# Switch experts in a two-layer transformer kernel: block inputs transposed one block ahead, outputs stored by slot and gathered by token, and an attention stage that starts from half of its operands

## The chip, the cores and the metric

The kernel runs on one core of one Trainium2 chip. The metric is the device time of one execution in microseconds (us). The core's engines are named as the profile names them: PE (TensorE, matmul and transpose), PEld (its weight loads), DVE (VectorE), ACT (ScalarE), POOL (GpSimd, which also issues the indirect DMAs) and SP (SyncE, which here only issues DMAs). L942 is line 942 of the kernel before.

## The reference, cut to what matters

The input x is [4, 1024, 128] (four images of 1024 tokens), all in float32. Two layers follow one another, each with two residual steps:

```python
x = x + L0_attn(layernorm(x))   # causal attention, 16 heads, rotary and content parts
x = x + L0_ffn(layernorm(x))    # "first experts"
x = x + L1_attn(layernorm(x))   # "second attention": 38 fixed offsets from 0 to 192
x = x + L1_ffn(layernorm(x))    # "last experts": top 2 of 8, rotations, a gate

def L0_ffn(x):                  # x is [4096, 128] here; 8 experts, FFN = 512
    route = softmax(x @ router_w + router_b)
    max_prob, max_ind = max(route), argmax(route)
    for e in range(8):
        a, g = split(x @ w1[e], 2)           # each 512 wide
        y = silu(a) * g @ w2[e]
        out = where(max_ind == e, y, out)
    return out * max_prob

def L1_attn(x):                 # 16 heads of 8
    q, k, v = x @ Wqkv.T + bqkv
    scores = q . k[n - offset] * scale + pos_bias[offset, head]
    out = softmax(scores) . v[n - offset]    # offsets before the start are left out
    return out * sigmoid(x @ Wgate.T + bgate) @ Wout.T + bout
```

## The kernel before

**Tiles.** x stays in SBUF for the whole program as 32 tiles of 128 tokens (P = 128, B = 4 images, NB = 8 tiles in an image, NT = 32). The four stages run one after the other: the first attention (to about 1150 us of the profiled span), the first experts (1150 to 1353 us), the second attention (to about 2000 us) and the last experts. In the stages that matter here PE executes its instructions in the order in which the program writes them (`manual_schedule`); the order on the other engines is set by the framework's scheduler when the program is built. Every engine executes its own instructions in order, so one that waits holds up all behind it.

**Sorting.** A token goes to one expert only. `route(t0, t1, room, ps_1)` sorts the tokens of the tiles t0 to t1 by expert into blocks of 128 slots in which all slots have the same expert. There are two groups, tiles 0 to 24 and 24 to 32 (`SORTED`); as each expert's share is rounded up to whole blocks, the first group has 24 + 7 = 31 blocks and the second 8 + 7 = 15, together 46. `route` is a generator: it normalises tokens (half of the tiles on DVE, half on POOL), transposes them on PE, stores them in DRAM (`xn_d`), computes the router's logits, and leaves `src_i` (for every slot the row of its token), `ex_i` (the expert of every block) and, inside it, `pos` (for every token its slot). The first group is sorted beside the first attention, the second one in pieces beside the first blocks.

**Blocks.** The stage's loop runs over the blocks j, with three of them in flight:

- `front(j)`: an indirect DMA on POOL gathers the block's 128 tokens from xn_d into xg (L932, 6 buffers); PE transposes xg (L937); DVE copies the transpose to xgT (L939); PE's sequencer loads the expert's number into a register (L940); PE multiplies xgT with the two halves of that expert's w1 into pa (L942) and pg (L949); ACT takes the silu of pa (sa, L947); DVE multiplies it with pg (hw, L954).
- `back(j)`, first half, one iteration later: PE transposes hw (L964) and ACT copies it to hT (L968). Second half, two iterations later: PE multiplies with w2 into y (L972), DVE copies y to ys (L978, 4 buffers), and an indirect DMA on POOL scatters ys to the rows of y_d that belong to its tokens (L979).

Between these, `piece()` runs one piece of the work in `aside`: first the sorting of the second group, then `tables()`, which loads what the second attention needs (by_query, by_key: 32 loads on SP, and weights), and, from the iteration after which the first group is complete, `outputs(b)` for the images 0 to 2. `outputs(b)` loads the 1024 rows of y_d of an image in order of tokens into yg (one DMA of 512 KB on SP, L1065) and adds yg times the router's probability (`mp`) to x on DVE, in eight instructions (L1074).

**Second attention.** Its work is cut into 16 units (b, g): image b, and a group g of four heads. `operands(n)` makes queries and keys of unit n. For the first unit of an image it begins with `shared(b)`: the layer norm's statistics, the normalised tokens xn (POOL, L1263), their transposes (PE L1267, copied to xnT by DVE L1268), the addition of b_out to x (POOL, L1271), the gate (L1279, L1280) and the values (L1284, L1288). Then come four matmuls (L1313), with qT (L1318) and kT (L1324) written by ACT. `maxima(n)` computes, in 16 steps, the scores sc (PE L1343) from which DVE takes the largest of every query (L1350); `turn` transposes these maxima (L1359, L1361, L1364). `attend(n)` computes the scores again with keys on the partitions (st, L1426), adds the bias (DVE L1435, sb), exponentiates (ACT L1439, pt) and multiplies with the values (av, L1451).

Ahead of the loop over the units, the program makes all operands of unit 0, then runs 22 steps of maxima (16 of unit 0, `lead` = 6 of unit 1). Beside these, the operands of unit 1 are made from the fifth step on, and the outputs of the first experts of the last image (`last`) are fetched and added from the seventh on:

```python
for _ in operands(0):
    pass
making = operands(1)
...
while done_m < steps + lead:
    if done_m >= 6:
        next(last, None)
    if done_m >= 4:
        for _ in making:
            break
```

Of the kernel before, what the change touches and what calls it, by code (L numbers as in the profile page):

```python
# [10 lines left out]
F32 = mybir.dt.float32  # L11
# [88 lines left out]
def fused_layers(ctx: ExitStack, tc: tile.TileContext, a: dict, out: bass.AP):  # L100
# [139 lines left out]

    mp = const.tile([P, NT], F32, tag="mp", name="mp")
    routed = []

    def route(t0, t1, room, ps_1):
# [4 lines left out]
        y_d = tc.dram_tile([1 + nt * P, D], F32, name=f"y_d{t0}")  # L249
        src_i = const.tile([P, nblk], I32, tag=f"src_i{t0}", name=f"src_i{t0}")  # L250
        ex_i = const.tile([P, nblk], I32, tag=f"ex_i{t0}", name=f"ex_i{t0}")
        inslot, idblk = room([P, nt, P], BF16), room([P, nt, 2, nblk], BF16)
# [13 lines left out]
        xna, xnT = room([P, 4, D]), room([P, 512])  # L266
        none = xna[0:1, 0, :]
# [3 lines left out]
        for b in range(t0 // NB, t1 // NB):  # L271
# [5 lines left out]
            for g in range(NB // 4):  # L277
                for q in range(4):
# [5 lines left out]
                yield  # L284
# [10 lines left out]
                yield  # L295
# [19 lines left out]
            nc.vector.reciprocal(mp[:, til], mp[:, til])  # L315

# [41 lines left out]
        pos_i = room([P, nt], I32)  # L358
# [35 lines left out]
        for g in range(nt // 4):  # L394
# [5 lines left out]
            yield  # L400
# [12 lines left out]
        routed.append((nblk, src_i, ex_i, xn_d, y_d))  # L413
# [503 lines left out]
    with ph0 as ph:  # L917
# [7 lines left out]

        def front(j):

            g = int(j >= routed[0][0])
            src_i, ex_i, xn_d = routed[g][1:4]
            k = j - g * routed[0][0]  # L930
            xg = pw.tile([P, D], F32, tag="xg", bufs=6)
            nc.gpsimd.indirect_dma_start(  # L932
                out=xg[:, :], out_offset=None, in_=xn_d[:, :],
                in_offset=bass.IndirectOffsetOnAxis(ap=src_i[:, k : k + 1], axis=0),
            )
            ps = ps_1.tile([P, 512], F32, tag="ps1")
            nc.tensor.transpose(ps[:, :P], xg, ident)  # L937
            xgT = pw.tile([P, P], F32, tag="xgT", bufs=3)
            nc.vector.tensor_copy(xgT, ps[:, :P])  # L939
# [17 lines left out]
        def back(j, hw, e):  # L957

            g = int(j >= routed[0][0])
            src_i, _, _, y_d = routed[g][1:]  # L960
            k = j - g * routed[0][0]
# [9 lines left out]
            for f in range(NFC):  # L971
# [7 lines left out]
            nc.gpsimd.indirect_dma_start(  # L979
                out=y_d[:, :], out_offset=bass.IndirectOffsetOnAxis(  # L980
                    ap=src_i[:, k : k + 1], axis=0
                ),
                in_=ys[:, :], in_offset=None,
            )
            yield

# [109 lines left out]
        for j in range(total + 2):  # L1096
            if j == first - 1:
                while len(routed) < 2:
                    piece()
# [634 lines left out]
```

## Time and profile before

| what | value |
|---|---|
| three runs | 2224.97, 2225.94, 2228.13 us; median 2225.94 us |
| profiled execution | 2226.58 us, its span 2224.8 us |
| mean granted clock of PE | 0.978 of full speed |
| busy share of the span | PE 92%, DVE 60%, PEld 49%, ACT 42%, POOL 20% |
| instructions | 31832 |
| DMA | 49.84 MB in 52836 packets |

By stage, in us of the span:

| stage | from, to | length | PE busy | DVE busy | POOL busy | granted clock |
|---|---|---|---|---|---|---|
| first attention, second half | 700 to 1150 | 450 | 431.5 | 232.4 | 93.1 | 0.99 |
| first experts | 1150 to 1353 | 203 | 170.8 | 79.1 | 92.7 | 0.96 |
| from there to the first st | 1353 to 1403 | 50 | 36.8 | 26.3 | 16.3 | 0.86 |
| second attention | 1403 to 2000 | 597 | 568.1 | 472.2 | 67.6 | 0.98 |
| last experts | 2000 to 2224.8 | 224.8 | 210.1 | 104.6 | 33.1 | 0.98 |

The profile is of one execution. "Busy" counts the time in which an engine executes instructions; a wait is put down to the instruction that waited and to the event that ended the wait, which is inferred from semaphores. The granted clock is the share of full speed that the chip's throttle allowed PE.

### The profile page before, as it was taken

The page shows a single profiled execution, that of the slowest core. Times are in us where ns is not written, and L with a number is a line of the kernel's source. Part 1 is how long each engine was busy: PE and PEld are TensorE (multiplying, and loading weights), DVE is VectorE, ACT ScalarE, POOL GpSimd, SP SyncE. Part 2 cuts the span into 40 slices and gives each one's busy share as a digit, 9 for nine tenths or more (in the row PEclk, how much of TensorE's full clock was granted, in tenths as well). Part 3 has the DMA queues.
Part 4 walks back from the last instruction along what each step waited for, and adds up shares of the span by engine and source line. Part 5 has one row for each costly group of instructions (what it writes and reads, how often), then busy time and mean ns, then how long its engine had stood idle before and what let it go on. Part 6 is the DMA issues. An engine that isn't in the chain of part 4 may idle for free. (4 is left out here: it accounts for less than half of the span.)

```text
span 2224.8 us, 31832 instructions
## 1 busy us (share of the span) xinstructions
PE 2048.0 (92%) x11540; PEld 1085.6 (49%) x11540; DVE 1345.9 (60%) x4098; ACT 923.8 (42%) x1491; POOL 443.8 (20%) x641
## 2 busy tenths in 40 slices
PE   5888999999999999999988887999999999989997
PEld 3654444444444444445335553555555555544453
DVE  5676746565555655555314343878778788674453
ACT  1112243344433444334543333454555545464553
POOL 3111122013210223013134543010000000151111
PEclk9999999999999999999999998999999999899998
DMA  3000000000000000020113220000000000031220
GB/s 68 1 1 1 1 2 1 2 1 1 1 1 1 1 1 1 6 79 28 36 37 109 77 56 18 2 1 2 2 1 2 1 2 2 13 97 55 86 82 15
DMA packets 52836, 49.84 MB, mean 22 GB/s; under 512 B 11555, under 2 KB 41480, under 8 KB 52680
## 3 DMA queue, kind: packets, MB, share of 16 engines
q1 hardware_dynamic: 48584, 40.90, 6.3%
q0 software_dynamic: 3216, 6.32, 1.1%
q8 instruction: 93, 1.52, 0.3%
q10 hardware_dynamic: 880, 0.57, 0.1%
q14 instruction: 63, 0.52, 0.1%
HBM read 39.85 MB, written 7.40 MB: 21 GB/s over the span
## 5 line engine op out<-in xcount | busy, mean ns | idle before, releaser
L707 ACT ACTIVATE pt<-st 128x1024 f32<-128x1024 f32 (+3 forms) x384 | 291.0, 808 | 381.9 <-PE st L700 376.3
L599 PE MATMUL sc<-kT,qT 64*128 64x512 f32 (+3 forms) x1536 | 412.5, 516 | 19.4 <-DVE mxs L615 9.6
L610 DVE CUSTOM_DVE_ANT_0 sc<-sc,cmask 128x512 f32<-128x512 f32 (+3 forms) x512 | 243.0, 512 | 142.0 <-PE sc L599 135.1
L700 PE MATMUL st<-qT,kT 64*128 64x512 f32 (+3 forms) x1536 | 309.9, 501 | 0.6 <-ACT pt L707 0.6
L599 PEld LDWEIGHTS sc<-kT,qT 64*128 64x128 f32 x1536 | 180.9, 189 | 199.6 <-DVE mxs L610 64.1
L1343 PE MATMUL sc<-kT,qT 64*128 64x320 f32 (+2 forms) x1024 | 261.3, 434 | 9.1 <-DVE mxs L1350 5.7
L1439 ACT ACTIVATE pt<-sb 128x640 f32<-128x640 f32 (+2 forms) x256 | 171.9, 683 | 217.2 <-DVE sb L1435 213.3
L1350 DVE CUSTOM_DVE_ANT_0 sc<-sc,by_query 128x320 f32<-128x320 f32 (+2 forms) x512 | 222.7, 473 | 53.4 <-PE sc L1343 50.8
L615 DVE TENSOR_REDUCE mxs<-sc 128x1 f32<-128x512 f32 x256 | 167.4, 687 | 116.6 <-PE sc L599 116.1
L711 POOL TENSOR_SCALAR_AFFINE_SELECT pt<-pt 128x256 f32<-128x256 f32 x256 | 102.9, 409 | 581.7 <-ACT pt L707 579.5
L700 PEld LDWEIGHTS st<-qT,kT 64*128 64x128 f32 x1536 | 151.6, 191 | 103.9 <-issue 68.8
L1426 PE MATMUL st<-qT,kT 64*128 64x320 f32 (+2 forms) x1024 | 191.0, 417 | 4.8 <-DMA qT<-mT 4.6
L1435 DVE TENSOR_TENSOR sb<-st,by_key 128x640 f32<-128x640 f32 (+2 forms) x256 | 182.3, 750 | 14.7 <-PE st L1426 12.0
L1343 PEld LDWEIGHTS sc<-kT,qT 64*128 64x128 f32 x1024 | 143.6, 186 | 82.9 <-DVE mxs L1350 31.6
L684 PE MATMUL av<-pt,va 128*32 128x512 f32 (+3 forms) x1536 | 168.5, 506 | 0.2 <-POOL pt L711 0.2
L1600 DVE TENSOR_TENSOR hd<-hd,wb 128x512 f32<-128x512 f32 x128 | 89.6, 710 | 101.8 <-ACT hd L1599 101.6
L1426 PEld LDWEIGHTS st<-qT,kT 64*128 64x128 f32 x1024 | 125.4, 189 | 31.5 <-DMA qT<-mT 9.9
L1699 PE MATMUL mT<-hd,ew 128*128 128x512 f32 x256 | 131.0, 595 | 2.7 <-DVE hd L1600 2.7
L1599 ACT ACTIVATE hd<-ps,eb 128x512 f32<-128x512 f32 x128 | 86.2, 686 | 103.6 <-PE ps L1594 91.7
L1594 PE MATMUL ps<-xnT,ew 128*128 128x512 f32 x192 | 98.0, 592 | 0.0
L1451 PE MATMUL av<-pt,va 128*32 128x320 f32 (+4 forms) x1280 | 90.9, 372 | 0.0
L954 DVE TENSOR_TENSOR hw<-sa,pg 128x512 f32<-128x512 f32 x46 | 31.6, 687 | 84.4 <-PE pg L949 75.8
(377 smaller groups left out, 2652.3 us busy)
## 6 DMA issues: line engine op xcount, KB each, us to landing
wb<-wt_d SPq DMA_DIRECT2D x64, 256.0 KB
w<-in_L_ffn_w SPq DMA_DIRECT2D x8, 512.0 KB
by_query<-bias_d SPq DMA_DIRECT2D x16, 160.0 KB
by_key<-bias_d SPq DMA_DIRECT2D x16, 160.0 KB
x<-in_L_attn_x SPq DMA_DIRECT2D x4, 512.0 KB
w<-in_L_ffn_w SPq DMA_DIRECT2D x8, 256.0 KB
ew<-in_L_ffn_ew SPq DMA_DIRECT2D x16, 128.0 KB
out<-mix SPq DMA_DIRECT2D x8, 256.0 KB
```

What stands on the lines that cost most here:

```text
L599: nc.tensor.matmul(sc[:, :n], qT[r0 : r0 + SLOT, pr, q * P : (q + 1) * P], kT[r0 : r0 + SLOT, pr, k0 : k0 + n], start=True, stop=True,)
L610: nc.vector.tensor_tensor_reduce(scs[hh][:, :n], scs[hh][:, :n], cmask[:, 512 - n :], 1.0, 2.0 * NEG, ALU.add, ALU.max, mx,)
L615: nc.vector.tensor_reduce(mx, scs[hh], AX.X, ALU.max)
L684: nc.tensor.matmul(av[hl * VSLOT : (hl + 1) * VSLOT, q0:], va[:, kb, h * VW : h * VW + VSLOT], pts[hl // 2][:, hl % 2, q0:], start=(kb == ...
L700: nc.tensor.matmul(st[:, hh, q0:], kT[r0 : r0 + SLOT, pr, kb * P : (kb + 1) * P], qT[r0 : r0 + SLOT, pr, q0:], start=True, stop=True,)
L707: nc.scalar.activation(pt[:, :, q0:], st[:, :, q0:], AF.Exp, scale=ATT_SCALE)
L1343: nc.tensor.matmul(sc[:, :w], qT[r0 : r0 + 2 * HSLOT, i * P : (i + 1) * P], kT[r0 : r0 + 2 * HSLOT, pl, k0 : k0 + w], start=True, stop=True,)
L1350: nc.vector.tensor_tensor_reduce(scs[hh][:, :w], scs[hh][:, :w], by_query[:, 4 * g + hl, :w][:, ::-1], 1.0, 2.0 * NEG, ALU.add, ALU.max, m ...
L1426: nc.tensor.matmul(st[:, hh, :w], kT[r0 : r0 + 2 * HSLOT, pl, q0 : q0 + P], qT[r0 : r0 + 2 * HSLOT, q0 : q0 + w], start=True, stop=True,)
L1435: nc.vector.tensor_tensor(sb[:, :, :w], st[:, :, :w], by_key[:, hs, WIN - w :][:, :, ::-1], ALU.add)
L1439: nc.scalar.activation(pt[:, :, :w], sb[:, :, :w], AF.Exp)
L1699: nc.tensor.matmul(mTs[k], ew2[:, e, f, :], hds.pop(n), start=False, stop=(s == steps - 1))
```

## The change

In the first experts:

- The slots' numbers `pos_i` of every token are kept. y_d now has one row for a slot (`nblk * P` rows): `back` stores ys with a plain DMA on SP into the block's 128 rows. `outputs(b, yg)` fetches the rows by token instead, with eight indirect DMAs on POOL for an image, one for a tile; their additions to x on DVE follow two pieces later.
- `front` is taken apart. `fetch(j)` gathers a block's tokens three blocks ahead; `turn(j + 1)` transposes and copies the next block's tokens behind pg of block j; `front(j)` begins with the load of the expert's number.
- The second group is sorted with `slack=2`: two buffers of normalised tokens instead of one, and an additional `yield` at some places, so that its work comes in more and smaller pieces. It has to be done three blocks before the second group's first block instead of one (`if j + ahead == first`).

In the second attention:

- The tokens of image 0 are normalised on DVE (the other images' still on POOL).
- `operands(0)` is interleaved with `shared(0)`: it makes queries and keys for the first 512 tokens right after their transposes, then those of the second 512, then the gate and the values. Two pieces of it run before the first step of maxima; the rest, and the operands of unit 1, go one piece to a step. The outputs of the last image still begin with the seventh step.

```diff
     mp = const.tile([P, NT], F32, tag="mp", name="mp")
     routed = []
-    def route(t0, t1, room, ps_1):
+    def route(t0, t1, room, ps_1, slack=1):
         nt = t1 - t0
         nblk = nt + E - 1
         xn_d = tc.dram_tile([1 + nt * P, D], F32, name=f"xn_d{t0}")
-        y_d = tc.dram_tile([1 + nt * P, D], F32, name=f"y_d{t0}")
+        y_d = tc.dram_tile([nblk * P, D], F32, name=f"y_d{t0}")
         src_i = const.tile([P, nblk], I32, tag=f"src_i{t0}", name=f"src_i{t0}")
         ex_i = const.tile([P, nblk], I32, tag=f"ex_i{t0}", name=f"ex_i{t0}")
+        pos_i = const.tile([P, nt], I32, tag=f"pos_i{t0}", name=f"pos_i{t0}")
         inslot, idblk = room([P, nt, P], BF16), room([P, nt, 2, nblk], BF16)
         inblk = room([P, nt, nblk])
         tri, allone, lane = room([P, P]), room([P, P]), room([P, P])
...
         unit = room([P, E * nt])
         nc.gpsimd.memset(unit, 1.0)
         lg, eq = room([P, NB, E]), room([P, NB, E])
-        xna, xnT = room([P, 4, D]), room([P, 512])
-        none = xna[0:1, 0, :]
+        xnas, xnT = [room([P, 4, D]) for _ in range(slack)], room([P, 512])
+        none = xnas[0][0:1, 0, :]
         nc.gpsimd.memset(none, 0.0)
         nc.sync.dma_start(out=xn_d[0:1, :], in_=none)
         yield
...
             mv, rstd = layer_norm(xb)
             yield
             for g in range(NB // 4):
+                xna = xnas[g % slack]
                 for q in range(4):
                     i = g * 4 + q
                     (nc.vector, nc.gpsimd)[q % 2].tensor_scalar(
                         xna[:, q, :], xb[:, i, :], mv[:, i, 0:1], rstd[:, i : i + 1],
                         ALU.subtract, ALU.mult,
                     )
-                yield
+                for _ in range(slack):
+                    yield
                 ps = ps_1.tile([P, 512], F32, tag="ps1")
                 for q in range(4):
                     nc.tensor.transpose(ps[:, q * P : (q + 1) * P], xna[:, q, :], ident)
...
         pos = room([P, nt])
         nc.vector.tensor_reduce(pos, upto.rearrange("p e t -> p t e"), AX.X, ALU.add)
         yield
-        pos_i = room([P, nt], I32)
         nc.vector.tensor_copy(pos_i, pos)
         slot_i = room([P, nt], I32)
         nc.vector.tensor_scalar(slot_i, pos_i, P - 1, None, ALU.bitwise_and)
...
         nc.vector.scalar_tensor_tensor(
             src_i, srcs[:, 0, :], float(P), srcs[:, 1, :], ALU.mult, ALU.add
         )
-        routed.append((nblk, src_i, ex_i, xn_d, y_d))
+        routed.append((nblk, src_i, ex_i, xn_d, y_d, pos_i))
         yield
...
         ps_y = ph.enter_context(tc.tile_pool(name="f_ps_y", bufs=1, space=PSUM, reuse_waits="tile"))
         ph.enter_context(tc.manual_schedule(engines={mybir.EngineType.PE}))
+        def of_group(j):
+            g = int(j >= routed[0][0])
+            return routed[g], j - g * routed[0][0]
+        xgs, xgTs = {}, {}
+        def fetch(j):
+            (_, src_i, _, xn_d, _, _), k = of_group(j)
+            xgs[j] = pw.tile([P, D], F32, tag="xg", bufs=6, name="xg")
+            nc.gpsimd.indirect_dma_start(
+                out=xgs[j][:, :], out_offset=None, in_=xn_d[:, :],
+                in_offset=bass.IndirectOffsetOnAxis(ap=src_i[:, k : k + 1], axis=0),
+            )
+        def turn(j):
+            ps = ps_1.tile([P, 512], F32, tag="ps1")
+            nc.tensor.transpose(ps[:, :P], xgs.pop(j), ident)
+            xgTs[j] = pw.tile([P, P], F32, tag="xgT", bufs=3, name="xgT")
+            nc.vector.tensor_copy(xgTs[j], ps[:, :P])
         def front(j):
-            g = int(j >= routed[0][0])
-            src_i, ex_i, xn_d = routed[g][1:4]
-            k = j - g * routed[0][0]
-            xg = pw.tile([P, D], F32, tag="xg", bufs=6)
-            nc.gpsimd.indirect_dma_start(
-                out=xg[:, :], out_offset=None, in_=xn_d[:, :],
-                in_offset=bass.IndirectOffsetOnAxis(ap=src_i[:, k : k + 1], axis=0),
-            )
-            ps = ps_1.tile([P, 512], F32, tag="ps1")
-            nc.tensor.transpose(ps[:, :P], xg, ident)
-            xgT = pw.tile([P, P], F32, tag="xgT", bufs=3)
-            nc.vector.tensor_copy(xgT, ps[:, :P])
+            (_, _, ex_i, _, _, _), k = of_group(j)
+            xgT = xgTs.pop(j)
             e = nc.tensor.value_load(ex_i[0:1, k : k + 1], min_val=0, max_val=E - 1)
             pa = ps_h.tile([P, 512], F32, tag="pa")
             nc.tensor.matmul(
...
         def back(j, hw, e):
-            g = int(j >= routed[0][0])
-            src_i, _, _, y_d = routed[g][1:]
-            k = j - g * routed[0][0]
+            (_, _, _, _, y_d, _), k = of_group(j)
             ps = ps_t.tile([P, 512], F32, tag="ps2")
             for f in range(NFC):
                 nc.tensor.transpose(
...
                 )
             ys = pw.tile([P, D], F32, tag="ys", bufs=4)
             nc.vector.tensor_copy(ys, y[:, :D])
-            nc.gpsimd.indirect_dma_start(
-                out=y_d[:, :], out_offset=bass.IndirectOffsetOnAxis(
-                    ap=src_i[:, k : k + 1], axis=0
-                ),
-                in_=ys[:, :], in_offset=None,
-            )
+            nc.sync.dma_start(out=y_d[k * P : (k + 1) * P, :], in_=ys)
             yield
         w_qk = b_qk = even = b_v = by_query = by_key = None
...
         def outputs(b, yg):
             g = int(b * NB >= SORTED[1][0])
-            t0, y_d = SORTED[g][0], routed[g][4]
-            nc.sync.dma_start(
-                out=yg,
-                in_=y_d[1:, :].rearrange("(t p) d -> p t d", p=P)[
-                    :, b * NB - t0 : (b + 1) * NB - t0, :
-                ],
-            )
+            t0, y_d, pos_i = SORTED[g][0], routed[g][4], routed[g][5]
+            for i in range(NB):
+                t = b * NB + i
+                nc.gpsimd.indirect_dma_start(
+                    out=yg[:, i, :], out_offset=None, in_=y_d[:, :],
+                    in_offset=bass.IndirectOffsetOnAxis(
+                        ap=pos_i[:, t - t0 : t - t0 + 1], axis=0
+                    ),
+                )
+                if i % 4 == 3:
+                    yield
+            yield
             yield
             for i in range(NB):
                 t = b * NB + i
...
         backs = {}
         first = routed[0][0]
         total = first + SORTED[1][1] - SORTED[1][0] + E - 1
+        ahead = 3
+        for j in range(ahead):
+            fetch(j)
+        turn(0)
         for j in range(total + 2):
-            if j == first - 1:
+            if j + ahead == first:
                 while len(routed) < 2:
                     piece()
+            if j + ahead < total:
+                fetch(j + ahead)
             if j < total:
                 backs[j] = back(j, *front(j))
+            if j + 1 < total:
+                turn(j + 1)
             piece()
             if j - 1 in backs:
                 next(backs[j - 1])
...
             gT = pk.tile([P, T], F32, tag="gT")
             va = pk.tile([P, NB, VCOLS], F32, tag="va")
             on = pk.tile([P, NB, D], F32, tag="on")
+            of[b] = xnT, gT, va, on
             nc.gpsimd.memset(va, 1.0)
             xb = x[:, b * NB : (b + 1) * NB, :]
             mv, rstd = layer_norm(xb)
...
                 ps = ps_1.tile([P, 512], F32, tag="ps1")
                 for q in range(4):
                     xn = pw.tile([P, D], F32, tag="xn_nat", bufs=4)
-                    nc.gpsimd.tensor_scalar(
+                    (nc.gpsimd if b > 0 else nc.vector).tensor_scalar(
                         xn, xb[:, c * 4 + q, :], mv[:, c * 4 + q, 0:1],
                         rstd[:, c * 4 + q : c * 4 + q + 1], ALU.subtract, ALU.mult,
                     )
...
             nc.gpsimd.tensor_tensor(
                 xb, xb, b_out.unsqueeze(1).to_broadcast([P, NB, D]), ALU.add
             )
-            of[b] = xnT, gT, va, on
             for c in range(T // 512):
                 tok = slice(c * 512, (c + 1) * 512)
                 xc = xnT[:, tok]
...
                 )
                 yield
+        def chunk_of_operands(n, c):
+            b, g = units[n]
+            xnT = of[b][0]
+            qT, kT = made[n]
+            tok = slice(c * 512, (c + 1) * 512)
+            for j in range(2):
+                ps = ps_1.tile([P, 512], F32, tag="ps1")
+                nc.tensor.matmul(
+                    ps, w_qk[:, j, 4 * g : 4 * g + 4, :].rearrange("p h s -> p (h s)"),
+                    xnT[:, tok], start=True, stop=True,
+                )
+                if j == 0:
+                    nc.scalar.activation(
+                        qT[:, tok], ps, AF.Identity, bias=b_qk[:, 0, g : g + 1],
+                        scale=L1_SCALE,
+                    )
+                else:
+                    for pl in range(2):
+                        nc.scalar.activation(
+                            kT[:, pl, tok], ps, AF.Identity,
+                            bias=b_qk[:, 1 + pl, g : g + 1], scale=even[:, pl : pl + 1],
+                        )
+                yield
         def operands(n):
             b, g = units[n]
-            if g == 0:
-                yield from shared(b)
-            xnT = of[b][0]
-            qT = pk.tile([P, T], F32, tag="qT", bufs=3)
-            kT = pk.tile([P, 2, T], F32, tag="kT", bufs=3)
-            made[n] = qT, kT
+            sharing = shared(b) if g == 0 else iter(())
+            if n > 0:
+                yield from sharing
+            made[n] = (
+                pk.tile([P, T], F32, tag="qT", bufs=3, name="qT"),
+                pk.tile([P, 2, T], F32, tag="kT", bufs=3, name="kT"),
+            )
             for c in range(T // 512):
...
+                if n == 0:
+                    next(sharing)
+                    if c > 0:
+                        yield
+                yield from chunk_of_operands(n, c)
+            yield from sharing
         def maxima(n):
...
         steps = 2 * NB
         lead = 6
         ph.enter_context(tc.manual_schedule(engines={mybir.EngineType.PE}))
-        for _ in operands(0):
-            pass
-        making = operands(1)
+        making = itertools.chain(operands(0), operands(1))
+        for _ in range(2):
+            next(making)
         maxs = (None for n in range(len(units)) for _ in maxima(n))
         done_m = 0
...
         while done_m < steps + lead:
             if done_m >= 6:
                 next(last, None)
-            if done_m >= 4:
-                for _ in making:
-                    break
-                if done_m == steps - 1:
-                    for _ in making:
-                        pass
+            next(making, None)
             next(maxs)
             done_m += 1
             pass_step()
...
```

## The prediction

> **What bounds the kernel now.** I read the page first (TensorE, PE, is 92% busy), then busy time in stretches of 20 us, to find where PE is not full. Both attentions and the last experts stay near full; the stage that the diff touches (first experts, about 1150 to 1353 us) and the 50 us behind it do not. The stretches (columns: stretch, its length, busy us of PE, weight load, DVE, ACT, POOL, granted clock, DMA share, GB/s):
>
> ```profile
> 1260.00:1280.00 20.00, 17.64 (x93) 11.43 (x92) 6.14 (x16) 6.45 (x11) 9.80 (x10) 1.00 0.12 37
> 1300.00:1320.00 20.00, 14.57 (x55) 8.70 (x56) 15.11 (x72) 5.61 (x9) 8.61 (x8) 0.83 0.34 92
> 1340.00:1360.00 20.00, 11.26 (x67) 8.02 (x65) 3.92 (x10) 3.73 (x7) 6.04 (x6) 0.92 0.05 20
> ```
>
> Even the undisturbed stretch has PE at 17.64 of 20, and no other engine is nearly as full: a latency, not an engine, sets the pace. The waits of this stage (waiter, whom it waited for, us, times, longest) say which:
>
> ```profile
> PE pa L942 <- DVE xgT L939: 27.5, 42, 4.1
> POOL y_d L979 <- DMA y_d<-ys,src_i: 13.6, 6, 3.7
> PE ps L1267 <- POOL xn L1263: 9.1, 4, 8.2
> ```
>
> One block in the timeline (start, us, engine, line, what; in brackets the idle time before):
>
> ```profile
> 1193.91 1.13 PE L942 MATMUL pa<-w,xgT 128*128 x2 [0.47 <-DVE xgT L939]
> 1194.88 1.02 PE L949 MATMUL pg<-w,xgT 128*128 x2
> 1195.73 0.60 PE L964 MATMUL ps<-ident,hw 128*128 128x128 f32 x4
> 1196.01 0.69 DVE L954 TENSOR_TENSOR hw<-sa,pg 128x512 f32<-128x512 f32 x1 [2.15 <-PE pg L949]
> 1196.17 1.06 PE L972 MATMUL y<-w,hT 128*128 x8
> 1197.06 0.27 PE L937 MATMUL ps<-ident,xg 128*128 128x128 f32 x1
> 1197.47 0.28 DVE L939 COPY xgT<-ps 128x128 f32<-128x128 f32 x1
> 1197.81 1.12 PE L942 MATMUL pa<-w,xgT 128*128 x2 [0.47 <-DVE xgT L939]
> ```
>
> The period is 1197.81 - 1193.91 = 3.90 us (3.895 over many), and the 0.75 us from the transpose of xg to the next pa is a round trip through DVE. From pa(0) at 1155.34 to pa(45) at 1346.22 the stage takes 190.9 us: 45 x 3.895 = 175.3, plus 7.4 in the first eight blocks (beside the second routing), 6.2 at pa(34) to pa(36) (1296.42, 1303.96, 1310.36: 13.9 for two periods, where DVE waits for yg), and 2.0 of small waits. Last y ends at 1352.7, the first score of the second attention starts at 1376.5, and its first st at 1402.9: 50.2 us.
>
> **Turning a block ahead.** The transpose (0.11 us of PE, by the 0.44 of four) moves behind pg; xgT is copied while PE does L964 and y. The round trip goes. New period: pa 0.855 (pg's value, 1195.73 - 1194.88; pa's 0.97 holds an unhidden weight load) + pg 0.855 + 0.11 + 0.44 + 0.89 = 3.15; with pa left at 0.97 it is 3.27; I take 3.17. What is late next is DVE: xgT(j+1) is queued behind hw(j). hw starts 2.10 after pa, now 1.99; + 0.69 + 0.28 + 0.06 = 3.02, 0.13 before it is needed. ACT has 1.2 us of work in a block, POOL one gather of 0.97: hidden.
>
> The load of the expert's number stood behind the transpose and under this round trip; now only y precedes it. Its row on PE's sequencer:
>
> ```profile
> L940 PEldq TENSOR_LOAD <-ex_i x46: 296/301/493, 1152.0 to 1343.0; - x46
> ```
>
> The last one starts at 1343.0, its pa at 1346.22: the sequencer is 3.2 us ahead, so its 0.30 us (0.52 with the register operations after it) stays hidden. The Trainium skill speaks against the change here: DMA: Bandwidth & Descriptors, "Latency and other measured facts", puts the floor of such a load at about 600 ns. Exposed, that would take back 45 x 0.6 = 27 us and turn my result into 5 us slower. The row (half the figure, and early) decides: 0.
>
> **Routing in smaller steps.** It doubles the buffer xna (the DVE wait of 2.34 and POOL wait of 2.76 us for the store of xn_d go) and spreads the pieces. Following the built order block by block, pa(2) falls to about 1163.0 (1165.47 before), pa(3) to 1166.7 (1172.31), pa(9) to 1189.9: 34.5 us = 9 x 3.17 + 6.0. Nearly the same overhead in another form: DVE's short operations still stand ahead of xgT(7), xgT(8) and xgT(9), and ACT's table loads stay. Other routing and table matmuls: 0.9.
>
> **Stores by slot.** 46 scatters of about 1 us leave POOL and become 46 stores on SP (0.35 each). Scatters waited for one another (3.85 us from start to start: 1350.14, 1353.99, 1357.84), which a 3.17 period would have run into; row blocks do not overlap, so that limit goes. SP's 32 loads of by_query and by_key (17.5 us) now stand between six stores: SP falls some 3 us behind, and ys has four buffers (12.7 us): 0.
>
> **Fetching by token.** Three loads of 512 KB become 24 gathers on POOL. The trace has their like, issued back to back:
>
> ```profile
> 1150.87 0.94 POOL L932 DMA_INDIRECT xg<-xn_d,src_i  x1 [0.30 <-issue]
> 1152.12 0.95 POOL L932 DMA_INDIRECT xg<-xn_d,src_i  x1 [0.30 <-issue]
> 1153.37 0.94 POOL L932 DMA_INDIRECT xg<-xn_d,src_i  x1 [0.30 <-issue]
> ```
>
> 1.25 us each, and these landed 2.3 us after their start (the trace's semaphore events). 24 of them are 30 us of POOL in a stretch where PE would need 19 for six blocks. In the built order 16 stand in one run on POOL after the fetch of block 40, then fetches 41 and 42, four more, fetch 43, four more. DVE has the 24 additions to x among its block work, so it waits for POOL in order, with hw and xgT behind: xgT(35) stands behind 2 gathers, xgT(36) behind 9, xgT(37) behind 16, xgT(38) behind 21, xgT(39) behind all 24.
> Zero is the end of ys(30), which completes the first group. Store: lands at about 2.2 (estimate from the 256 KB store of xn_d, waited for 2.70). Fetch 40 waits for the transpose of block 34 and ends at 3.0, so gather 1 starts at 3.3. xgT(36): 3.3 + 8 x 1.25 + 2.3 + 1.4 (addition, statistics, hw, copy) = 17.0; free running wants 9.2. xgT(37): 3.3 + 15 x 1.25 + 2.3 + 1.5 = 25.9. xgT(38): 24th issue of POOL, 3.3 + 23 x 1.25 + 2.3 + 0.6 = 35.0. The 27th lands at 38.1; ys(35), statistics, hw(37) and hw(38) before xgT(39) make 42.6, and pa(40) starts near 46.5 where free running had 21.9. Loss 24.5 us, in place of 6.2.
> This counts little for the clock, where the skill warns (TensorE: Matmul & The Clock Gate, Part 1: an idle window of some 3.4 us halves the clock). The trace agrees:
>
> ```profile
> 1303.96 2.08 PE L942 MATMUL pa<-w,xgT 128*128 x2 [4.12 <-DVE xgT L939]
> ```
>
> Taking half speed on each of four restarts gives 4 x 3.2 = 13 us; but the gathers pace those blocks at 9 us, so only the last restart is paid: 1.0, in the 46.5.
>
> Block stage after: 45 x 3.17 + 6.0 + 0.9 + 24.5 = 174.0; gain 16.9.
>
> **Second attention.** x is normalised on DVE (8 x 0.35) instead of behind scatters on POOL (0.79 each, PE waits 8.2), and maxima begin with half of the operands. But 8 gathers of the last images' outputs stand on POOL with the addition of b_out (2.45) after the second, and DVE has their additions ahead of or among the first three pairs of maxima. From the last y: store 2.6, gathers start at 2.7 and 3.95, b_out 5.2 to 7.7, the others 8.0 to 14.2, landed 16.5, third maxima done near 18.5. The rest of operands(0) and operands(1), eight pieces, now go beside steps 4 to 11. Before, four pieces with five steps took 8.8 (1380.25 to 1389.07); eight take 16 to 17. Then 11 steps of 0.92 = 10.1: first st at about 45, against 50.2. Gain 5; bounds 0 (another table load late) and 12 (gathers not waited for).
>
> **Sum.** The profiled execution took 2226.58 (span 2224.8), 0.64 over the median 2225.94. 16.9 + 5 = 22 less: 2204.6 for it, 2204 for the median. Nothing else moves: the first attention's order is unchanged.
>
> **Rivals.**
> (1) The transposes gain less: DVE has only 0.13 us to spare, and a period of 3.4 gives 10 us less: 2214. For it: one sum of five modelled ends; against it: slack everywhere else.
> (2) Gathers cost less, because DVE or POOL gets ahead: a pace of 0.97 saves 26 x 0.28 = 7 us, no stall at all 24: 2180 to 2197. Against it: the 0.30 gap is in every pair above.
> (3) Slower than before: gathers from y_d run slower on POOL than those from xn_d. Place: the 26 intervals behind ys(30). They use up the 22 us from a pace of 1.25 + 22/26 = 2.1 us on; if each waited for the one before as scatters do (3.85), 68 us are added: 2272. Against it: they write separate slices, and the built program waits only for the eighth before.
> (4) No net change: the exposed register load in part.
>
> **Numbers.** Forecast 66% (2195 to 2213); (1) 12%; (2) 8%; (3), slower, 11%; (4) within 0.2% 3% (0.2%, 4.5 us, is about what a measurement of this kernel tells from none). Faster 0.86. Leaving out (3), (4) and the outer parts of (1) and (2): 2193 to 2217.
>
> **What would show it.** Right: pa to pa near 3.2 us in the middle blocks with no wait for xgT; DVE waiting over 20 us for DMA yg<-y_d; gathers 1.25 apart; first st 45 us after the last y. Wrong: PE idle before pa in every block; gathers further apart than 2 us; or pa(34) to pa(40) done in 25 us.

## The result, and the profile after

The changed kernel takes 2199.85 us (median of four runs, 2195.81 to 2203.28); the kernel before took 2226.93 us (four runs, 2224.97 to 2228.13). The ratio is 0.9878, 95% interval 0.9862 to 0.9894: 27 us less. Forecast were 22 us less (2204, range 2193 to 2217). The profiled execution is the slowest of the four, 2203.28 us with a span of 2201.6, which is 23.2 below the span of before; the parts below add up to these 23.2 us, not to the 27 between the medians.

Read from the starts of pa (block 0 to block 45), the end of the last y and the first st in both timelines, in us:

| part | before | forecast | after |
|---|---|---|---|
| start to pa(0) | 1155.3 | 1155.3 | 1154.0 |
| pa(0) to pa(9) | 42.5 | 34.5 | 33.3 |
| pa(9) to pa(34) | 98.6 | 80 | 80.4 |
| pa(34) to pa(40) | 30.3 | 43.5 | 42.0 |
| pa(40) to pa(45) | 19.5 | 15.9 | 15.8 |
| pa(45) to the end of the last y | 6.5 | 6.5 | 6.4 |
| last y to first st | 50.2 | 45 | 51.9 |
| first st to the end | 821.9 | 821.9 | 818.0 |

The first stretches to compare are of 20 us again (columns: stretch, its length, busy us of PE, weight load, DVE, ACT, POOL, granted clock, DMA share, GB/s): an undisturbed one and one beside the gathers.

```profile
1230.00:1250.00 20.00, 20.00 (x106) 13.34 (x105) 7.30 (x19) 7.36 (x13) 5.63 (x6) 1.00 0.29 73
...
1270.00:1290.00 20.00, 12.05 (x43) 7.40 (x41) 9.46 (x31) 4.23 (x6) 15.12 (x17) 0.74 0.23 59
```

The undisturbed stretch is now full: PE 20.00 of 20. A block in the timeline (start, us, engine, line, what; in brackets the idle time before):

```profile
1242.36 1.02 PE L963 MATMUL pa<-w,xgT 128*128 x2
...
1243.22 1.02 PE L970 MATMUL pg<-w,xgT 128*128 x2
...
1244.08 0.27 PE L953 MATMUL ps<-ident,xg 128*128 128x128 f32 x1
...
1244.19 0.60 PE L983 MATMUL ps<-ident,hw 128*128 128x128 f32 x4
1244.35 0.69 DVE L975 TENSOR_TENSOR hw<-sa,pg 128x512 f32<-128x512 f32 x1 [1.50 <-PE ps L953]
...
1244.63 1.06 PE L991 MATMUL y<-w,hT 128*128 x8
...
1244.95 0.28 DVE L955 COPY xgT<-ps 128x128 f32<-128x128 f32 x1
...
1245.52 1.02 PE L963 MATMUL pa<-w,xgT 128*128 x2
```

No bracket stands on a PE row: the period is 1245.52 - 1242.36 = 3.16 us (before 3.895, forecast 3.17). xgT ends at 1245.23, the next pa starts at 1245.52. The register load stays early (its last one at 1323.2, the last pa at 1325.37):

```profile
L961 PEldq TENSOR_LOAD <-ex_i x46: 297/302/495, 1150.6 to 1323.2; - x46
```

The stall behind block 34 is where the forecast put it. In the waits from 1263 to 1310 us (waiter, whom it waited for, us, times, longest) and in the timeline before pa(36):

```profile
DVE x L1093 <- DMA yg<-y_d,pos_i: 20.2, 20, 4.1
...
PE pa L963 <- DVE xgT L955: 11.8, 4, 3.9
```

```profile
1279.21 0.94 POOL L1081 DMA_INDIRECT yg<-y_d,pos_i  x1 [0.30 <-issue]
1279.21 0.35 DVE L1093 SCALAR_TENSOR_TENSOR x<-yg,mp,x 128x128 f32<-128x128 f32 x1 [0.66 <-DMA yg<-y_d,pos_i]
...
1280.46 0.94 POOL L1081 DMA_INDIRECT yg<-y_d,pos_i  x1 [0.30 <-issue]
1280.53 0.35 DVE L1093 SCALAR_TENSOR_TENSOR x<-yg,mp,x 128x128 f32<-128x128 f32 x1 [0.76 <-DMA yg<-y_d,pos_i]
...
1281.00 0.67 DVE L975 TENSOR_TENSOR hw<-sa,pg 128x512 f32<-128x512 f32 x1
1281.58 0.28 DVE L955 COPY xgT<-ps 128x128 f32<-128x128 f32 x1
...
1281.92 2.07 PE L963 MATMUL pa<-w,xgT 128*128 x2 [3.88 <-DVE xgT L955]
```

DVE follows POOL's 1.25 us step by step; hw and xgT stand behind the additions. 42.0 us for six blocks of 3.16 leaves 23.0 us of stall (forecast 24.5).

The beginning of the second attention is what the forecast had wrong: 51.9 us, not 45. In the waits from 1332 to 1384 us DVE stands at image 3's additions, and PE at the maxima behind them:

```profile
DVE x L1093 <- DMA on<-y_d,pos_i: 7.5, 6, 3.0
...
PE ps L1334 <- DVE mxs L1389: 5.2, 3, 2.9
```

The stretches, columns as above:

```profile
1335.73:1343.73 8.00, 5.89 (x16) 2.92 (x14) 4.69 (x14) 3.04 (x5) 6.83 (x6) 0.71 0.17 43
1343.73:1351.73 8.00, 4.97 (x8) 1.51 (x8) 3.96 (x23) 3.39 (x5) 6.58 (x8) 0.50 0.10 25
1351.73:1361.73 10.00, 9.43 (x24) 4.56 (x24) 2.91 (x11) 2.30 (x3) 0.00 (x0) 0.50 0.00 0
1361.73:1371.73 10.00, 9.24 (x36) 3.76 (x36) 5.55 (x21) 3.30 (x5) 0.00 (x0) 0.97 0.00 1
```

The third row is the one to see: PE is busy 9.43 of 10 us at a granted clock of 0.50, and 24 of its instructions fall into these 10 us, where the next 10, at 0.97, hold 36.

### The profile page after: what moved, and what is told of

It reads as the page before. It is cut to its first block, busy times and chain, and to the rows that moved or that the text cites. A ratio compares the mean times of both kernels' runs of the same rounds, so it can differ in the third digit from the quotient of the medians.

```text
span 2201.6 us, 31856 instructions
## 1 busy us (share of the span) xinstructions
PE 2046.7 (93%) x11540; PEld 1088.2 (49%) x11540; DVE 1349.1 (61%) x4106; ACT 926.4 (42%) x1493; POOL 419.6 (19%) x619
## 4 chain that ended last, share of the span: by engine, by line
PE 79%; DVE 11%; issue 3%; POOL 2%; ACT 2%; DMA 2%; SPq 0%; POOLq 0%; ACTq 0%; DVEq 0%
PE sc L608 15%; PE st L709 12%; PE sc L1382 7%; PE av L693 7%; PE mT L1734 5%; PE ps L1629 5%; PE st L1465 5%; PE ps L479 3%; PE ps L1334 3%; PE av L1490 2%; DVE sc L1389 2%; DVE sb L1474 2%; PE psk L546 1%; DVE mxs L624 1%; PE pa L963 1%
## 5 line engine op out<-in xcount | busy, mean ns | idle before, releaser
L608 PE MATMUL sc<-kT,qT 64*128 64x512 f32 (+3 forms) x1536 | 412.5, 516 | 19.3 <-DVE mxs L624 9.6
L1382 PE MATMUL sc<-kT,qT 64*128 64x320 f32 (+2 forms) x1024 | 266.3, 442 | 8.1 <-DVE mxs L1389 5.6
L1334 PE MATMUL ps<-xnT,w_qk 128*128 128x512 f32 x128 | 73.7, 660 | 6.7 <-DVE mxs L1389 5.9
```

Of the source, the lines that this page charges most:

```text
L608: nc.tensor.matmul(sc[:, :n], qT[r0 : r0 + SLOT, pr, q * P : (q + 1) * P], kT[r0 : r0 + SLOT, pr, k0 : k0 + n], start=True, stop=True,)
L1382: nc.tensor.matmul(sc[:, :w], qT[r0 : r0 + 2 * HSLOT, i * P : (i + 1) * P], kT[r0 : r0 + 2 * HSLOT, pl, k0 : k0 + w], start=True, stop=True,)
```

## The experiments

All are read by the same parts. Kernels under one heading shared a chip and its runs of the kernel before; the chips differ a little (the changed kernel was run again beside the second group: 0.9903, 0.9881 to 0.9925), so totals are compared as ratios, and parts of us by the traces.

| kernel | pa(0)-pa(9) | pa(9)-pa(34) | pa(34)-pa(40) | pa(40)-pa(45) | last y to first st | ratio to before (95%) |
|---|---|---|---|---|---|---|
| before | 42.5 | 98.6 | 30.3 | 19.5 | 50.2 | 1 |
| changed | 33.3 | 80.4 | 42.0 | 15.8 | 51.9 | 0.9878 (0.9862 to 0.9894) |
| turn_scatter | 33.5 | 80.5 | 35.0 | 16.5 | 57.1 | 0.9904 (0.9887 to 0.9922) |
| old_begin | 34.2 | 80.4 | 47.0 | 15.8 | 46.7 | 0.9907 (0.9889 to 0.9925) |
| begin_only | 42.5 | 98.6 | 30.1 | 19.5 | 55.7 | 1.0025 (1.0015 to 1.0035) |
| slack1 | 34.5 | 80.2 | 47.0 | 15.8 | 47.8 | 0.9926 (0.9910 to 0.9942) |
| after_again | 33.5 | 80.4 | 41.9 | 15.8 | 52.0 | 0.9903 (0.9881 to 0.9925) |
| last_late | 34.1 | 80.4 | 41.8 | 15.8 | 40.5 | 0.9864 (0.9844 to 0.9884) |
| spread | 33.3 | 80.4 | 19.0 | 15.8 | 38.9 | 0.9786 (0.9760 to 0.9811) |
| ts_best | 33.3 | 80.4 | 21.4 | 20.8 | 44.8 | 0.9819 (0.9801 to 0.9837) |
| spread3 | 34.1 | 80.4 | 19.0 | 15.8 | 44.9 | 0.9796 (0.9774 to 0.9817) |
| slack1_again | 34.4 | 80.2 | 41.9 | 15.8 | 53.3 | 0.9918 (0.9896 to 0.9940) |

### First group: one part of the change undone, or done alone

**turn_scatter** keeps the scatters and loads of before:

```diff
-            nc.sync.dma_start(out=y_d[k * P : (k + 1) * P, :], in_=ys)
+            nc.gpsimd.indirect_dma_start(
+                out=y_d[:, :], out_offset=bass.IndirectOffsetOnAxis(
+                    ap=src_i[:, k : k + 1], axis=0
+                ),
+                in_=ys[:, :], in_offset=None,
+            )
...
+            nc.sync.dma_start(out=yg, in_=...)   # one load of 512 KB for an image, as before
```

> The changed kernel with outputs stored and read back as before (a scatter by token on POOL, one load of 512 KB for an image on SP); tokens are still turned a block ahead, the second attention begins in the new way. Theory A (the prediction's): scatters wait for one another 3.85 us from start to start, so they become the pace: pa(9) to pa(34) 96 us (before 98.6, changed kernel 80.4), block stage pa(0) to pa(45) about 181 us, total about 2217. Rival B: the 3.85 was only the pace of the blocks, closer scatters overlap: pa(9) to pa(34) 80 us, block stage about 155 us, total about 2191, better than the changed kernel.

Theory A, the prediction's, falls: pa(9) to pa(34) takes 80.5 us with scatters as well. The trace of before could have told it. The prediction quoted its last three scatters, 3.85 apart; further up, where POOL catches up after having fallen behind, they follow closer, and so they do in turn_scatter (first fence before, second turn_scatter):

```profile
1243.26 0.99 POOL L979 DMA_INDIRECT y_d<-ys,src_i  x1 [0.74 <-issue]
...
1246.29 0.99 POOL L979 DMA_INDIRECT y_d<-ys,src_i  x1 [0.77 <-issue]
...
1249.30 0.99 POOL L979 DMA_INDIRECT y_d<-ys,src_i  x1 [0.74 <-issue]
```

```profile
1244.76 0.98 POOL L998 DMA_INDIRECT y_d<-ys,src_i  x1 [0.76 <-issue]
...
1247.78 0.98 POOL L998 DMA_INDIRECT y_d<-ys,src_i  x1 [0.76 <-issue]
...
1250.80 0.98 POOL L998 DMA_INDIRECT y_d<-ys,src_i  x1 [0.76 <-issue]
```

3.02 us from start to start, just below the block's 3.16. This is the pace at which they catch up, not the pace of all: in the same 25 blocks some of turn_scatter's scatters start up to 6.43 us behind the one before, with POOL waiting up to 4.2 us for it, and PE is not held up. So stores by slot add nothing to the middle blocks, and the gain there is that of the taken-apart `front`: turning ahead, together with fetching ahead, which no run separates from it. Rival B's total (2191) is not reached either: DVE stands 13.6 us at the additions, waiting for the first load of yg (35.0 for six blocks), and the beginning takes 57.1, as the last scatters, 3.85 apart here too, delay image 3.

**old_begin** undoes the new beginning of the second attention:

```diff
-        making = itertools.chain(operands(0), operands(1))
-        for _ in range(2):
-            next(making)
+        for _ in operands(0):
+            pass
+        making = operands(1)
...
-                    (nc.gpsimd if b > 0 else nc.vector).tensor_scalar(
+                    nc.gpsimd.tensor_scalar(
```

> The changed kernel with the second attention's beginning as before (all operands of unit 0 ahead of the maxima, image 0 normalised on POOL); first experts as changed. Theory A (the prediction's): the new beginning is worth 5 us: last y to first st 57 us, total 2205. Rival B: half clock and the waits for gathers ate it: in the old order the first maximum comes at about 22 us, behind the 8 gathers and b_out on POOL, and the first st at about 47.5 us (changed kernel 51.9), total about 2195.5, faster than the changed kernel.

By the part, rival B: 46.7 us against 51.9. But this does not show that the new beginning loses 5 us. slack1 (below) has the new beginning; it took 47.8 us in its profile on the same chip, and 53.3 in one on another. Its two profiles differ in how long PE stays at half clock there, 13.7 us in the first and 23.9 in the second. Against 47.8, the old beginning is 1.1 us shorter. So beside the gathers the new beginning gains nothing, and what it loses was not settled. The total (0.9907) does not settle it either: 5 us more are lost at pa(34) to pa(40), to a stop that is discussed below.

**begin_only** is the kernel before with the new beginning alone, the reverse of that diff.

> The kernel before with the new beginning of the second attention alone (no gathers there: image 3 comes with one load on SP). DVE has the eight additions of image 3 ahead of the first maximum: last scatter landed about 8, load 10.5, additions done about 13.5 us behind the last y. Theory A (the new beginning gains by itself, at full clock): 14 + 16.5 + 11 = 41.5 us from the last y to the first st (before 50.3), total 2218. Rival B (the interleaved pieces run at half clock, as in the changed kernel, 26.6 in place of 16.5): about 51.5 us, total 2226 to 2229.

Rival B, and worse: 55.7 us against 50.2 of before, and the total is 0.25% above it, in 22 runs against 27. DVE has the additions of image 3 ahead of the first maximum and waits 10.0 us for their load, behind the last scatters; PE stands still for 9.5 us behind them, and the granted clock is 0.50 for 24 us (1357.7 to 1381.6).

**slack1** sorts the second group in the pieces of before:

```diff
-        aside = [route(*SORTED[1], Room(room), ps_1, slack=2), tables()]
+        aside = [route(*SORTED[1], Room(room), ps_1), tables()]
```

> The changed kernel with the second group sorted in the pieces of before (one buffer of normalised tokens, no additional yields). Theory A (the prediction's: the same overhead in another form): pa(0) to pa(9) 36 us at most (33.3 with the smaller pieces), total within 3 us of the changed kernel's. Rival B: the smaller pieces are a real part of the gain: pa(0) to pa(9) stays near the 42.5 us of before, total 9 us above the changed kernel's.

Theory A by this part: pa(0) to pa(9) 34.5, 1.2 us above the changed kernel. The smaller pieces are worth about 1 us. The total is higher by more (0.9926, and 0.9918 when run again, against 0.9878 and 0.9903), which these parts explain only in part.

### The stop beside the gathers

In old_begin and slack1, pa(34) to pa(40) took 47.0 us, 5 more than in the changed kernel. In the waits of slack1 from 1266 to 1313 us:

```profile
ACT sa L968 <- remote: 17.6, 1, 17.6
DVE ys L997 <- remote: 14.6, 1, 14.6
...
PE y L991 <- DVE ys L997: 11.8, 1, 11.8
```

ys had its y since 1274.8 and started at 1296.34; sa had its pa since 1282.4 and started at 1297.78. No instruction of these three engines ran from 1284.9 to 1296.3, while POOL went on issuing gathers. "remote" means that the profile has no event for what ended the wait. Both kernels had run on one chip. The changed kernel was run again beside the second group, and slack1 beside the third, each on another chip.

> The changed kernel once more, as a second profile of it on the chip of the next three. Theory A (the stop of 11 to 12 us of PE, DVE and ACT together that old_begin and slack1 show beside the gathers is a matter of the execution, not of those edits): pa(34) to pa(40) lies anywhere from 42 us (first profile) to 47 us, last y to first st near 52 us. Rival B (the stop belongs to those two kernels): 42 us again. Total 0.986 to 0.990 of the kernel before.

> slack1 once more. In its first profile and in old_begin's, PE, DVE and ACT stood still together for 11 to 12 us beside the gathers; in two profiles of the changed kernel and in last_late, with the same gathers, they did not. Theory A (it comes with the chip of that call, not with the kernel): pa(34) to pa(40) 42 us here. Rival B (it comes with the kernel): 47 us again. pa(0) to pa(9) 34.5 us in both.

Theory A in both: 41.9 us, no stop. As slack1 has it once and once not, the kernel alone does not bring it; whether the chip or the single execution does, and its cause, stay open.

### Second group: the two stalls taken away

**last_late** moves image 3's outputs from the maxima to the first unit:

```diff
         while done_m < steps + lead:
-            if done_m >= 6:
-                next(last, None)
             next(making, None)
...
                 next(maxs, None)
+                next(last, None)
                 two = [next(attending), next(attending)]
```

> The changed kernel with the outputs of image 3 fetched and added beside the first unit's attend steps, not beside the maxima ahead of it (their additions on DVE pinned in program order). Theory A (image 3's gathers and additions delay the first maxima, and the idle time they make drops the clock to half for 20 us): first maximum without waits, pieces at full clock, last y to first st 36 to 38 us in place of 51.9, total about 14 us below the changed kernel's. Rival B (pieces and maxima in alternation leave PE idle by themselves and stay at half clock): 46 us or more.

Theory A, though at 40.5 us in place of 51.9, where 36 to 38 were expected. The scheduler kept image 3's gathers where they were (their starts lie 2.8 to 13.8 us behind the last y, in both kernels); only the eight additions moved, to 1386 us and later. Its stretches (same columns), the first beginning 4 us behind the last y as above:

```profile
1331.82:1339.82 8.00, 6.79 (x23) 2.71 (x21) 1.33 (x9) 3.92 (x6) 6.84 (x6) 0.88 0.14 43
1339.82:1351.82 12.00, 10.65 (x46) 4.94 (x48) 7.12 (x26) 4.36 (x7) 6.45 (x8) 1.00 0.06 16
1351.82:1368.32 16.50, 14.86 (x65) 7.93 (x63) 12.48 (x55) 4.93 (x7) 0.00 (x0) 1.00 0.01 1
```

The granted clock is 1.00 where the changed kernel had 0.50. The same eight pieces take 19.3 us (1338.03 to 1357.37) where they took 26.4 in the changed kernel. What is gone are DVE's waits for image 3's gathers ahead of the first maxima, and with them the longer of PE's own waits for maxima (the matmul of the pieces; 5.2 us in the changed kernel, as shown above):

```profile
PE ps L1336 <- DVE mxs L1391: 1.2, 2, 0.6
```

Of the 11.4 us gained at the beginning, the first two units give back 4.0 (32.6 + 33.3 us against 29.8 + 32.1), as DVE has eight additions more there. The total is 7.7 us below the changed kernel's on that chip (2192.88 against 2200.56), where 14 were expected.

**spread** goes on from there: images 0 and 1 in the block stage, one gather to a piece and none in every fourth, each addition four gathers behind its gather; images 2 and 3 beside the first units. `keep_in_program_order` holds an instruction behind what the program wrote before it on its engine (the remarks behind # are not in the program).

```diff
+            todo = [(b, i, yg) for b, yg in images for i in range(NB)]
+            for k in range(len(todo) + lag):
+                if k < len(todo):
+                    gather(*todo[k])         # kept in program order on POOL
+                if k >= lag:
+                    add(*todo[k - lag])      # kept in program order on DVE
+                yield
+                if rest and k % (rest - 1) == rest - 2:
+                    yield
```

> As last_late, and the outputs of the first experts spread: in the block stage only images 0 and 1, one gather to a piece and none in every fourth, each addition four gathers behind its gather; images 2 and 3 beside the first units of the second attention; gathers and additions pinned in program order on POOL and DVE. Theory A (the 23 us stall behind block 34 is DVE waiting in order for gathers that come 1.25 us apart): pa(34) to pa(40) 20 to 22 us in place of 42, pa(40) to pa(45) 16 to 17.5, last y to first st 36 to 38, total about 2175 (0.977 of before). Rival B (DVE has no room among the blocks: each addition ahead of hw costs its 0.35 us, or sixteen more additions lengthen the units): 8 to 10 us of it lost, about 2184.

Theory A: pa(34) to pa(40) is 18.95 us, six periods, without a stall; DVE's room among the blocks is enough for additions that are due. The total is 0.9786, 46 us less than before on that chip (2177.08 against 2223.08). Rival B is right of the units alone: the first three are 9.5 us longer than in the changed kernel (31.6 + 36.3 + 43.3 against 29.8 + 32.1 + 39.8).

**ts_best** is turn_scatter with the additions held behind their loads in the same way, and image 3 as in last_late.

> turn_scatter (scatter by token, loads of 512 KB on SP) with the additions to x pinned and spread over the blocks that follow, and image 3 loaded and added beside the first unit's attend steps. Theory A (turning ahead is the whole gain of the block stage; stores by slot bring none, as scatters follow one another in 3.02 us where a block takes 3.16): pa(9) to pa(34) 80.5 us, pa(34) to pa(40) 20 to 22 (35.0 in turn_scatter), last y to first st 36 to 38, total about 2174, as good as spread or better. Rival B (scatters and fetches on one queue fall behind near the end, or the loads wait for the last scatter so long that DVE stops): pa(34) to pa(45) above 45 us, total above 2184.

Between the two: 21.4 us for pa(34) to pa(40), so turning ahead with additions that are not early does nearly all; but the last blocks take 20.8 (15.8 with stores by slot) and the beginning 44.8. Behind block 34 DVE's ys waits 17.0 us in all for the DMA of earlier scatters, which still hold its buffers; that this makes the 20.8 was not tested alone. Here stores by slot with spread gathers are better: 0.9786 against 0.9819.

### Third group: all three images in the block stage

**spread3** has `range(3)` images, a lag of 6 and no rest in the block stage, image 3 beside the first unit.

> spread with image 2's outputs too in the block stage: two gathers to a block, each addition six gathers behind its gather; image 3's stay beside the first unit of the second attention. In spread POOL had ended its gathers 26 us behind pa(34) where the last y ends 41.6 us behind it, and units 1 to 3 were 9.5 us longer than in the changed kernel by sixteen additions. Theory A: pa(34) to pa(45) stays at 35 us, last y to first st near 39, the units lose 4 to 5 us in place of 9.5; total about 2172 (0.976 of before or less). Rival B: two gathers and a fetch are 3.75 us of POOL in a block of 3.16; DVE waits for the last gathers: pa(40) to pa(45) 18 us or more and later first maxima, total no better than spread's 2177.

The block stage is as expected, pa(34) to pa(45) 34.7 us. This is the cleanest test of the stall: POOL issues the same 24 gathers in the block stage, one DMA every 1.25 us, and the last one later than in the changed kernel (35.4 us behind pa(34), there 32.8), but the additions stand six gathers behind theirs. The fetches of blocks stand elsewhere among the gathers too, but by the waits PE stood for no fetched block here in either kernel. In its timeline:

```profile
1276.06 0.94 POOL L946 DMA_INDIRECT xg<-xn_d,src_i  x1 [0.30 <-issue]
...
1277.31 0.94 POOL L1080 DMA_INDIRECT yg<-y_d,pos_i  x1 [0.30 <-issue]
...
1277.79 0.28 DVE L955 COPY xgT<-ps 128x128 f32<-128x128 f32 x1
...
1277.99 0.60 DVE L1091 SCALAR_TENSOR_TENSOR x<-yg,mp,x 128x128 f32<-128x128 f32 x2
...
1278.35 1.02 PE L963 MATMUL pa<-w,xgT 128*128 x2
```

Two additions run behind xgT without a wait, in DVE's idle time ahead of the next hw. The stall goes from 23.0 us to none. The first three units lose 4.2 us in place of 9.5 (31.5 + 34.6 + 39.8). But the beginning takes 44.9 us where 39 were expected: image 2's trailing additions come first, and the granted clock is 0.50 from about 4 to 16 us behind the last y. So the total is no better than spread's (0.9796), as rival B had it, though not by the waits that it named.

## Why the prediction was right, and where it was not

- **The period** (3.17): 3.16 measured, by pa at pg's length and DVE in time. The gain of the middle blocks, 18.2 us, and most of that of the first nine, 9.2, are the taken-apart `front`: turn_scatter keeps both without stores by slot. That it is the turning and not the fetching rests on the trace of before, where PE's wait was for xgT. Rival (1), a period of 3.4, did not come.
- **The register load** (cost 0): right. The load's row is as before, 302 ns and 2.2 us ahead of the last pa. Rival (4), an exposed load, did not come.
- **Routing in smaller steps** (6.0 us of overhead in the first nine blocks, nearly that of before): 33.3 - 9 x 3.16 leaves 4.9; by slack1, 1.2 us of the gain are the smaller pieces.
- **The stall of 24.5 us at the gathers**: 23.0 measured; gathers 1.25 us apart, DVE's waits 20.2 us, pa restarts of 2.07. spread3 shows the cause to be the place of the additions on DVE, not POOL's time. So the gathers' price of 24.5 us was no price of gathering: rival (2)'s outer case, no stall at all, is what an order with later additions reaches.
- **"Scatters ... which a 3.17 period would have run into"**: false. Scatters do wait for one another, but three rows at the end of the trace were read as the least distance; further up stood 3.02. The number cost the sum nothing, since the change removes the scatters, but it gave stores by slot a merit that turn_scatter denies them in these blocks.
- **The beginning of the second attention** (a gain of 5): wrong, a loss of 1.6. The sum was 18.5 + 16.5 + 10.1 us; measured are 14.5 (third maxima done behind the last y), 26.4 (eight pieces, 1346.2 to 1372.6) and 11.0. The term that failed is "eight take 16 to 17". It was scaled from four pieces at full clock, and two things were wrong with it. The clock: it was 0.50 until 1362.3, and the same pieces take 19.3 us in last_late at 1.00, so half clock cost about 7.1. The scaling: 19.3 is 2.8 above 16.5 even at full clock; the eight include pieces of the gate and the values, which the four did not. The prediction weighed the clock for the restarts of four blocks, and did not ask it here. That image 3's additions delay the maxima is shown by last_late.
- **The clock there**: the Trainium skill (TensorE: Matmul & The Clock Gate, Part 1) makes an idle window of some 3.4 us the condition for half clock. In this trace less was enough: the clock was 0.50 from 1335 to 1338 behind PE waits of 0.64 and 0.67 us, and again from 1341.8 on behind one of 1.63 (before 1340.80); the longest came later, 2.89 (before 1346.18). Where they differ, the measurement decides. Nor do waits alone explain when it comes back: two of 0.58 and 0.57 us followed (before 1349.99 and 1353.79), then PE was, by the profile, busy without a break to 1362.3, 8.5 us, still at 0.50. In slack1's first profile the clock was back 21 us behind the last y, in the changed kernel 30.5, and last_late, with the same first two waits, was back at 1.00 at 1333.7 and stayed there. What decides how long half clock lasts was not found.
- **Outside the sum**: pa(0) came 1.4 us earlier, and 3.9 us were gained behind the first st. The 1.4 need not be of an edit: two profiles of the changed kernel differ by more (1154.0 and 1150.2). Of the 3.9 no cause was found. The largest single difference, from the first st of unit 14 to that of unit 15, is 37.8 us before and 32.5 after; it goes with the new beginning (36.0 in old_begin, 32.7 in begin_only), but other units take part of it back, and old_begin gains nearly as much behind the first st (818.4 us).

The gain of 23.2 us between the two spans is thus 19.5 from the block stage (forecast 16.9), 1.6 lost at the beginning (forecast 5 gained), 1.4 and 3.9 from outside: the mechanism of the block stage was right, but the total came out close partly by luck, as an error of 6.6 us at the beginning was made up by 2.6 more in the blocks and 5.3 that the forecast did not have. Rival (3), gathers that slow each other, did not come: POOL issued them 1.25 apart throughout. Of the prediction's four signs of being right three came (the period, DVE's wait, the gathers' pace); the first st at 45 us did not.

## What to carry to other kernels

When a load is turned into many small gathers, look at what consumes them on an engine that executes in order: emitted early, the consumers hold all work behind them at the pace of the gathers; emitted a few gathers late and held there, they cost these blocks nothing, and 23 us of stall went to none with the same 24 gathers. Small pieces of TensorE work interleaved behind waits have to be costed at both clocks: here eight pieces took 26.4 us at half clock for most of the time and 19.3 at full clock. The least distance of two DMAs is read from the closest pair in the whole trace, not from the last ones. And a part that a run of the same kernel can move by 5 us (47.8 and 53.3 in slack1) is not settled by one profile of each side.

## What the runs showed of the hardware that was not expected

Half clock does not need a long pause, and it can outlast the pauses: in the changed kernel, behind PE waits of 0.6 to 2.9 us, the granted clock stayed at 0.50 for 20 us, the last 8.5 of them with PE busy without a break. In last_late, with the same pieces and without the waits for image 3's gathers, it was 1.00 from 1333.7 us on. Profiles of one kernel can differ in this: slack1 came back to full clock 21 us behind the last y in one and 33 us in the other. And on one chip PE, DVE and ACT stood still together for 11 to 12 us beside a run of gathers, in two kernels, with their operands ready as far as the profile shows; in four other profiles with the same gathers (two of the changed kernel, last_late, slack1 run again) it did not come.
